# A layer of two mixtures of experts around attention: the first routing in written order, its slot sums in two PSUM banks, and one shared expert moved to another stage

## The chip, the cores and the metric

The kernel runs on one core of a Trainium2 chip. The metric is the device time of one execution in microseconds (us). Before the change three runs gave 1568.17, 1572.17 and 1578.36 us, so the median is 1572.17 us. Engines are named as the profile names them: PE multiplies matrices (PEld is its weight load), DVE does elementwise work and reductions, ACT evaluates functions and copies, POOL issues the gathers and the scatter-adds, and SP issues the other transfers.

## The reference, cut to what matters

The input is X of 4 sequences x 512 tokens x 512 values, all float32. The same mixture of experts (weights and router) is applied before and after an attention layer:

```python
x = L0_attn_X
x = x + 0.5 * _L0_ffn_ref(_layernorm(x, axis=-1), ...)
x = x + _L0_attn_ref(_layernorm(x, axis=-1), ...)
x = x + 0.5 * _L0_ffn_ref(_layernorm(x, axis=-1), ...)

# _L0_ffn_ref: 64 experts of width 192, each token in 6 of them
router_logits = x @ gate_w
topk_w, topk_ids = _grouped_topk(router_logits, bias)     # 8 groups of 8 experts; the best 4 groups, then the best 6
y = _routed_moe(x, topk_w, topk_ids, w_gate, w_up, w_down)
shared = jax.nn.silu(x @ ws_gate) * (x @ ws_up) @ ws_down
return (y + shared).reshape(orig_shape)
```

The reference's capacity is 2 * (512 * 6 // 64) = 96 slots for each expert. A token beyond an expert's 96th is dropped from it. The attention has 16 heads of 32 values and a rotary embedding of half of them.

## The kernel before, in words

**Stages.** Times are those of the profiled execution. First routing and most of the first shared expert (0 to 142 us); the first 32 pairs of experts (157 to 452); the rest of the first shared expert, then the projections to queries, keys and values; for each sequence b a *sums* stage (row maxima and sums of exponentials) and a *context* stage (probabilities times values), beside which run the projections of the next sequence and the second layer's routing of the one before; a last routing (1179 to 1229); the second 32 pairs of experts (to about 1542); a final addition.

**Routing (class `Route`).** A token tile is 128 tokens, a sequence has four. `begin` computes the layer norm's statistics of a sequence on DVE. `row` normalises a tile on ACT and stores it to `xn_d` in HBM; it has two buffers in the first routing. `turn` transposes the tile on PE and copies it on ACT, `score` multiplies it with the router's weights and takes a tanh on ACT (0.22 us). `choices` finds the experts of a whole sequence on DVE, in seven parts that a generator separates with `yield`; `choose` runs all seven. `count` finds each token's slot with two PE products (`pp`) and five DVE operations. `digits` compares the slot number's digits on DVE, giving tiles A and V for a pair of token tiles; in the first routing each has one buffer. `tokens` scales one half of V by the token's number with two ACT operations. `spread` multiplies A and V on PE into a bank `o` for each half of the groups (16 small products), and DVE adds the two into `acc`: index parts as they are, parts that say which pair of tiles it was times the pair's number. After eight pairs `finish` turns `acc` into the slot lists `en`, by which POOL gathers the experts' rows.

**Shared expert.** `gate` multiplies a tile with both input weights on PE (128x384, eight records of the trace), takes a tanh on ACT and two products on DVE (`product`); `turn_h` transposes the result on PE and copies it on ACT; `down` multiplies with the output weights on PE (`so`) and adds into x on DVE. `store` issues what waits to be stored.

**What sets the order.** PE's instructions stand in the order in which they are written. In the first routing only SP does so besides; ACT and DVE are ordered there by a scheduler. A list `steps` gives the places of the choices, counts and slot sums among the steps of the shared expert: in a loop over sequences g of 0 to 2 and five steps i, each step transposes tile i - 1's gate product, gates tile i, transposes and scores tile i of sequence g + 2, does what `steps` says, stores, issues one weight load and one clearing of the output (`some(1)`), and multiplies down tile i - 1. Weights of the first five pairs of experts (15 transfers of 768 KB) and 17 clearings of 256 KB and more are issued from this loop. The gathers wait for the rows, the routing weights and the cleared last rows of `xn_d`.

In the attention stages ACT and DVE are in written order as well. A list of pieces, each with a nominal cost, is worked off beside the 16 rounds of each stage:

```python
def long(self, keep=0):
    if sum(p[0] >= 1.0 for p in self.left) > keep:
        self.short()
        self.take()
```

A round of `sums` or `context` takes at most one piece of cost 1.0 or more, and up to two shorter ones around it; `sums` keeps two long pieces back, which `work.all()` runs behind the last round. `scored`, `gated` and `queued` give the pieces of the second layer's routing of a sequence: scores, the shared expert (four gates), and count with slot sums. Before the change `scored(b - 1)`, `gated(b - 1)` and `queued(b - 1)` run in context stages 1 and 2; those of the third sequence are in the fourth sums stage and, for `queued`, in the fourth context stage.

Of the kernel before, what the change touches and what calls it, by code (L numbers as in the profile page):

```python
# [9 lines left out]
F32 = mybir.dt.float32  # L10
# [7 lines left out]
P = 128  # L18
# [13 lines left out]
CAP = 96  # L32
# [50 lines left out]
def macaron_kernel(ctx: ExitStack, tc: tile.TileContext, X, ln_w, ln_b, W_in, W_out, gate_w, bias,  # L83
# [173 lines left out]
    class Route:  # L257


        def __init__(self, layer):  # L260
            self.layer = layer
            self.before_g = const.tile([P, E], BF, tag=f"before{layer}", name="before_g")
            nc.vector.memset(self.before_g, 0.0)

            self.acc = const.tile([CAP, G, 2 * SB, EG], BF, tag="acc", name="acc")
# [164 lines left out]
        def tokens(self, g, i):  # L430

            V = self.AV[g, i][1]
            for j, part in enumerate((part_1, part_2)):
                r = slice(j * G, (j + 1) * G)
                nc.scalar.activation(V[:, r, 0, :], V[:, r, 1, :], AF.Copy, scale=part)

        def spread(self, g, i, psum=None):

            (A, V), n, h = self.AV.pop((g, i)), 2, G // 2
            for k in range(2):  # L440
                o = (psum or self.psM).tile([P, 512], F32, tag="ps", name="o")
                ov = o[:CAP].rearrange("p (g w e) -> p g w e", g=h, e=EG)
                for q in range(h):
                    for j in range(n):
                        r = j * G + k * h + q
                        nc.tensor.matmul(ov[:, q].rearrange("p w e -> p (w e)"),
                                         lhsT=A[:, r].rearrange("p a e -> p (a e)"),
                                         rhs=V[:, r].rearrange("p w b -> p (w b)"), start=j == 0, stop=j == n - 1)
                to, pair = self.acc[:, k * h:(k + 1) * h], (g * TPB + i) // n
# [9 lines left out]
        def finish(self, psum=None):  # L459

            Z = self.rp.tile([CAP, 2, SB, G, EG], BF, tag="Z", name="Z", bufs=1)
            nc.vector.tensor_tensor(Z.rearrange("p v b g e -> p (v b) g e"), self.acc.rearrange("p g w e -> p w g e"),
                                    same.unsqueeze(1).unsqueeze(1).to_broadcast([CAP, 2 * SB, G, EG]), ALU.mult)
# [163 lines left out]
    with ExitStack() as s:  # L627
# [4 lines left out]
        with ExitStack() as f:  # L632
            rp = f.enter_context(tc.tile_pool(name="rp0", bufs=2))
            f.enter_context(tc.manual_schedule(engines={mybir.EngineType.SP}))
# [13 lines left out]
            route.use(rp, psA, psD, 2)  # L648
            route.xp = rp, 2 * TPB
            route.begin(0, xs[0])  # L650

            for t in range(2 * TPB + 1):
                g, i = divmod(t, TPB)
                if t == TPB - 1:
                    with tc.issue_after(route.begun):
                        route.begin(1, xs[1])
                if g < 2:
                    route.row(g, xs[g], i)
                    route.turn(g, i)
                if t > 0:  # L660
                    route.score(*divmod(t - 1, TPB))
                if t == TPB:
                    for later in range(2, B):
                        with tc.issue_after(route.begun):
                            route.begin(later, xs[later])
                    route.choose(0)
# [22 lines left out]
            steps = [lambda: route.choose(1), lambda: count(0), lambda: spread(0, 0), lambda: spread(0, 2), None,  # L689
                     lambda: (route.choose(2), count(1)), lambda: spread(1, 0), lambda: spread(1, 2), lambda: count(2),  # L690
                     None, lambda: (route.choose(3), spread(2, 0)), lambda: spread(2, 2), lambda: count(3),
                     lambda: spread(3, 0), lambda: spread(3, 2)]
            for g in range(B - 1):
# [33 lines left out]
    with ExitStack() as s:  # L727
# [167 lines left out]
        def gated(b):  # L895
# [5 lines left out]

            pieces = []
# [4 lines left out]
            return pieces  # L907

        def queued(b, chosen):

            def last():
                route.down(b, xs[b], TPB - 1)
# [10 lines left out]
            pieces = [(0.3, lambda: route.turn_h(b, TPB - 1)), (1.7, last)]  # L923
# [114 lines left out]
        for b in range(B):  # L1038
            if b > 0:
# [6 lines left out]
                else:  # L1046
                    work.add(pieces + [rest, rest] + early_rows(b - 1) + scored(b - 1, chosen) + gated(b - 1))
# [106 lines left out]
```

## Time and profile before

| | us |
|---|---|
| median of three runs | 1572.17 |
| profiled execution | 1571.97 |
| its span, first to last instruction | 1570.3 |
| PE busy | 1407.7 (90%) |
| DVE busy | 619.1 (39%) |
| ACT busy | 602.8 (38%) |
| POOL busy | 351.0 (22%) |
| mean granted clock of PE | 0.935 |
| routing's slot lists ready | 142.2 |
| first gather starts | 150.0 |
| first transpose of gathered rows | 157.35 |
| third context stage | 944.2 to 1031.3 |
| fourth sums stage | 1031.4 to 1120.8 |
| fourth context stage | 1121.3 to 1179.1 |

The span runs from the first to the last instruction of one profiled execution. Busy time counts each engine by itself; matrix products are pipelined, so a busy PE is not a PE at its peak. A row of instructions gives start, duration, engine, line, operation, tiles and count; in square brackets stands how long the engine sat idle before it and what ended that. A row of waits gives who waited for whom, the total, the number of times and the longest.

### The profile page before, as it was taken

How to read it: one execution, taken by the hardware profiler on the slowest of the kernel's cores; microseconds unless marked ns; L12 is line 12 of the kernel's file. 1: busy time of each engine (PE TensorE's matmuls, PEld its weight loads, DVE VectorE, ACT ScalarE, POOL GpSimd, SP SyncE). 2: the span in 40 equal slices, each digit the busy share in tenths (PEclk: the TensorE clock that was granted, in tenths of full speed). 3: DMA queues.
4: the chain of work that ended last, by engine and by line, in shares of the span. 5: the costliest groups of instructions: out<-in, count | busy, mean ns of one | idle time of the engine just before them, and what ended most of it. 6: DMA issues, size and time to landing. Idle time of an engine off the chain costs nothing.

```text
span 1570.3 us, 22935 instructions
## 1 busy us (share of the span) xinstructions
PE 1407.7 (90%) x9008; PEld 801.8 (51%) x9008; DVE 619.1 (39%) x1528; ACT 602.8 (38%) x1153; POOL 351.0 (22%) x321
## 2 busy tenths in 40 slices
PE   4785999999998999999899999998898799999990
PEld 4552877766653443334343334434334477777760
DVE  7575212221117566166144851465515412221110
ACT  4431112111112487568635775457562112121110
POOL 2001355554434000000000000000000245555535
PEclk9998899999998996999899998996998799999995
DMA  5377699999999300000000010000006489999989
GB/s 195 132 243 263 191 336 329 333 332 335 337 269 155 122 1 1 1 1 0 22 31 7 1 52 36 31 1 27 31 1 229 131 268 336 333 334 329 335 252 122
DMA packets 127035, 254.57 MB, mean 162 GB/s; under 512 B 15800, under 2 KB 32312, under 8 KB 126928
## 3 DMA queue, kind: packets, MB, share of 16 engines
q1 hardware_dynamic: 87216, 192.96, 35.0%
q0 software_dynamic: 39424, 59.97, 17.8%
q8 instruction: 72, 1.18, 0.3%
q14 instruction: 35, 0.29, 0.1%
q10 hardware_dynamic: 288, 0.16, 0.0%
HBM read 202.21 MB, written 56.95 MB: 165 GB/s over the span
## 4 chain that ended last, share of the span: by engine, by line
PE 55%; ACT 5%; DVE 4%; DMA 4%; issue 2%; POOL 1%; SPq 0%; POOLq 0%; ACTq 0%; DVEq 0%
PE pq L810 11%; PE gu L548 6%; PE sct L968 5%; PE sc L937 5%; PE cx L991 4%; PE sct L972 4%; PE ps_t L200 4%; PE po L859 3%; DMA w<-in_L_ffn_w_up_dram 3%; PE eo L567 3%; PE so L507 3%; PE gu L207 3%; PE gu L552 2%; PE eo L570 2%; ACT sc L945 1%
## 5 line engine op out<-in xcount | busy, mean ns | idle before, releaser
L525 POOL DMA_INDIRECT xr<-xn_d,en x128 | 119.7, 936 | 898.1 <-DVE sg L214 726.5
L548 PE MATMUL gu<-bT,w 128*128 128x96 f32 x2048 | 245.8, 278 | 9.4 <-DMA w<-in_L_ffn_w_up_dram 9.2
L548 PEld LDWEIGHTS gu<-bT,w 128*128 128x128 f32 x2048 | 238.5, 194 | 12.8 <-issue 12.7
L945 ACT ACTIVATE sc<-sc,nmq 128x512 f32<-128x512 f32 x256 | 168.9, 660 | 56.8 <-DVE nmq L940 51.1
L810 PE MATMUL pq<-w,lT 128*128 128x512 f32 x384 | 182.4, 623 | 5.5 <-ACT lT L201 2.7
L940 DVE TENSOR_REDUCE nmq<-sc 128x2 f32<-128x1024 f32 x128 | 151.3, 1221 | 76.9 <-PE sc L937 76.9
L575 POOL DMA_INDIRECT total<-ob,en x96 | 138.6, 1444 | 163.1 <-ACT ob L574 120.0
L574 ACT ACTIVATE ob<-eo,xr 96x512 f32<-96x512 f32 x128 | 80.6, 679 | 185.9 <-PE eo L570 182.6
L979 ACT ACTIVATE pT<-sct 128x1024 f32<-128x1024 f32 x128 | 124.2, 1022 | 63.7 <-PE sct L972 63.4
L559 DVE SCALAR_TENSOR_TENSOR sg<-sg,gu 128x288 f32<-128x288 f32 x64 | 29.1, 454 | 302.5 <-ACT sg L558 226.7
L558 ACT ACTIVATE sg<-gu 128x288 f32<-128x288 f32 x64 | 26.3, 411 | 314.8 <-PE gu L554 307.0
L567 PE MATMUL eo<-w,hT 128*96 128x512 f32 x256 | 125.3, 612 | 0.0
L810 PEld LDWEIGHTS pq<-w,lT 128*128 128x128 f32 x384 | 72.7, 198 | 97.7 <-issue 83.7
L201 DVE COPY bT<-ps_t 128x384 f32<-128x384 f32 x128 | 65.5, 552 | 136.1 <-PE ps_t L200 119.9
L937 PE MATMUL sc<-kT,qT 32*128 32x512 f32 x512 | 98.9, 720 | 12.7 <-ACT sc L945 12.0
L554 PE MATMUL gu<-bT,w 128*64 128x96 f32 x1024 | 98.7, 250 | 0.0
L552 PE MATMUL gu<-bT,w 128*64 128x96 f32 x1024 | 98.7, 250 | 0.0
L207 PE MATMUL gu<-wsgu,xT 128*128 128x384 f32 x256 | 94.4, 516 | 1.7 <-ACT ob L574 1.4
L968 PE MATMUL sct<-qT,kT 32*128 32x512 f32 x512 | 92.2, 664 | 3.1 <-ACT pT L979 3.1
L972 PE MATMUL sct<-nmT,pick 4*128 4x512 f32 x512 | 87.1, 629 | 5.1 <-ACT nmT L957 5.1
L552 PEld LDWEIGHTS gu<-bT,w 128*64 128x64 f32 x1024 | 86.7, 137 | 6.1 <-issue 0.2
L554 PEld LDWEIGHTS gu<-bT,w 128*64 128x64 f32 x1024 | 86.7, 137 | 0.0
(159 smaller groups left out, 1636.0 us busy)
## 6 DMA issues: line engine op xcount, KB each, us to landing
w<-in_L_ffn_w_gate_dram SPq DMA_DIRECT2D x64, 768.0 KB
w<-in_L_ffn_w_up_dram SPq DMA_DIRECT2D x64, 768.0 KB
w<-in_L_ffn_w_down_dram SPq DMA_DIRECT2D x64, 768.0 KB
total<-zero SPq DMA_DIRECT2D x39, 256.0 KB
xn_d<-xn SPq DMA_DIRECT2D x32, 256.0 KB
x<-in_L_attn_X_dram SPq DMA_DIRECT2D x16, 256.0 KB
x<-total POOLq DMA_DIRECT2D x16, 256.0 KB
out_dram<-x SPq DMA_DIRECT2D x16, 256.0 KB
```

The lines of the kernel that those rows point to most:

```text
L207: nc.tensor.matmul(gu[:rows, :2 * F].rearrange("p (w f) -> p w f", w=2), lhsT=bT[:, c, :], rhs=weights[:, :, c, :], start=c == 0, stop=c = ...
L548: nc.tensor.matmul(g[:, k, :], lhsT=w[:, k, c, f:f + P], rhs=x[:, c, :], start=c == 0, stop=c == DC - 1)
L552: nc.tensor.matmul(g[:FC, 2, :], lhsT=w[:, 0, c, P:F], rhs=xa[:, c, :], start=c == 0, stop=c == DC - 1)
L554: nc.tensor.matmul(g[FC:, 2, :], lhsT=w[:, 1, c, 0:FC], rhs=xb[:, c, :], start=c == 0, stop=c == DC - 1)
L567: nc.tensor.matmul(eos[k][:CAP], lhsT=hT[:, k, :], rhs=wd[:, 2 * k, :], start=True, stop=False)
L575: nc.gpsimd.indirect_dma_start(out=total[layer][k], in_=ob, in_offset=None, out_offset=bass.IndirectOffsetOnAxis(ap=en[:, e:e + 1], axis=0 ...
L810: nc.tensor.matmul(pq, lhsT=lTs[i][:, c, :], rhs=win[n][:, c, :], start=c == 0, stop=c == DC - 1)
L937: nc.tensor.matmul(scs[j // 2][:, j % 2, :], lhsT=qT[b][rows, c, q * P:(q + 1) * P], rhs=kT[b][rows, c, :], start=True, stop=True)
L940: nc.vector.tensor_reduce(nmv[:, q, 2 * pair:2 * pair + 2, c], scs[pair], AX.X, ALU.max, negate=True)
L945: nc.scalar.activation(scs[j // 2][:, j % 2, :], scs[j // 2][:, j % 2, :], AF.Exp, bias=nmq[:, q, j * DH + c:j * DH + c + 1], accum_out=sm ...
L968: nc.tensor.matmul(scs[j // 2][:, j % 2, :], lhsT=kT[b][rows, c, kt * P:(kt + 1) * P], rhs=qT[b][rows, c, :], start=True, stop=False)
L972: nc.tensor.matmul(scs[j // 2][:, j % 2, :], lhsT=pick[rows, c, :], rhs=nmT[b][rows, :], start=False, stop=True)
```

## The change

In the first routing ACT and DVE are put in written order too, and the order is written anew: all statistics first; rows one tile ahead; weight loads and clearings from the second tile on; in each step of the shared expert the gate without its products, the next sequence's transpose and score, then count (step 0) or slot sums (steps 1 and 2), then one part of the next choice, the gate's products, and another part. `count` and the slot sums of the last sequence stand behind the loop.

The slot sums of the first routing are held in the two banks of pool `psB`: a product of zeros opens each bank, the products of all eight pairs add to it, the pair's number is applied on ACT to the second half of V in `tokens`, and `finish` reads the two banks. `acc` is left to the second layer.

In the attention stages `gated` now ends with the last transpose and down projection, which were in `queued`. `gated(1)` moves from the third context stage to the fourth sums stage, where it takes the place of two empty pieces; two empty pieces stand ahead of `queued` in the second and third context stages.

```diff
-        def use(self, rp, psT, psM, xn_bufs, dig_bufs=1, last=False):
+        def use(self, rp, psT, psM, xn_bufs, dig_bufs=1, last=False, held=None):
...
+            self.sums = held and [held.tile([P, 512], F32, tag="ps", name="o") for _ in range(2)]
+            for o in self.sums or []:
+                nc.tensor.matmul(o[:CAP], lhsT=zero.bitcast(BF)[:, :CAP], rhs=zero.bitcast(BF)[:, :512], start=True, stop=False)
...
+            if self.sums:
+                nc.scalar.activation(V[:, :, 1, :], V[:, :, 1, :], AF.Copy, scale=float((g * TPB + i) // 2))
...
-                o = (psum or self.psM).tile([P, 512], F32, tag="ps", name="o")
+                o = self.sums[k] if self.sums else (psum or self.psM).tile([P, 512], F32, tag="ps", name="o")
...
+                                         start=j == 0 and not self.sums,
+                                         stop=j == n - 1 and (not self.sums or (pair, q) == (pairs - 1, h - 1)))
+                if self.sums:
+                    continue
...
+            for at, part in parts:
+                n = part.shape[1]
+                nc.vector.tensor_tensor(Z.rearrange("p v b g e -> p (v b) g e")[:, :, at:at + n, :],
...
-            f.enter_context(tc.manual_schedule(engines={mybir.EngineType.SP}))
+            f.enter_context(tc.manual_schedule(engines={mybir.EngineType.SP, mybir.EngineType.Activation, mybir.EngineType.DVE}))
...
-            route.use(rp, psA, psD, 2)
+            route.use(rp, psA, psD, 2, held=psB)
...
+            for g in range(B):
+                route.begin(g, xs[g])
+            route.row(0, xs[0], 0)
+            for t in range(2 * TPB + 1):
+                if t + 1 < 2 * TPB:
+                    g, i = divmod(t + 1, TPB)
+                    route.row(g, xs[g], i)
+                if t < 2 * TPB:
+                    route.turn(*divmod(t, TPB))
+                if t > 0:
+                    route.score(*divmod(t - 1, TPB))
+                    some(1)
+                if t == TPB:
+                    route.choose(0)
...
-                        route.gate(g, i)
+                        route.gate(g, i, 1)
                         if ahead:
                             route.turn(ahead, i)
                             route.score(ahead, i)
                             if i + 1 < TPB:
                                 route.row(ahead, xs[ahead], i + 1)
-                    step = steps.pop(0)
-                    if step:
-                        step()
+                        if i == 0:
+                            count(g)
+                        elif i < 3:
+                            spread(g, 2 * i - 2)
+                        choice(g + 1, 1)
+                        route.product(g, i)
+                        choice(g + 1, 1)
+                    if i > 0:
+                        route.down(g, xs[g], i - 1)
                     route.store()
                     some(1)
-                    if i > 0:
-                        route.down(g, xs[g], i - 1)
+            count(B - 1)
+            for i in range(0, TPB, 2):
+                spread(B - 1, i)
             route.finish()
...
-            return pieces
+            return pieces + [(0.3, lambda: route.turn_h(b, TPB - 1)), (1.7, last)]
...
-                    work.add(pieces + [rest, rest] + early_rows(b - 1) + scored(b - 1, chosen) + gated(b - 1))
+                    work.add(pieces + gated(b - 2) + early_rows(b - 1) + scored(b - 1, chosen) + gated(b - 1))
...
-                work.add(scored(b - 1, chosen) + gated(b - 1) + queued(b - 1, chosen))
+                work.add(scored(b - 1, chosen) + (gated(b - 1) if b == 1 else []) + [rest, rest] + queued(b - 1, chosen))
```

More of the change, by code (lines that the diff above doesn't have):

```diff
@@ L263, in __init__ @@
             nc.vector.memset(self.before_g, 0.0)
-            self.acc = const.tile([CAP, G, 2 * SB, EG], BF, tag="acc", name="acc")
+            self.acc = const.tile([CAP, G, 2 * SB, EG], BF, tag="acc", name="acc") if layer else None
             self.en = const.tile([CAP, E], U32, tag="en", name="en")
@@ L435, in tokens @@
                 nc.scalar.activation(V[:, r, 0, :], V[:, r, 1, :], AF.Copy, scale=part)
+            if self.sums:
+                nc.scalar.activation(V[:, :, 1, :], V[:, :, 1, :], AF.Copy, scale=float((g * TPB + i) // 2))
         def spread(self, g, i, psum=None):
             (A, V), n, h = self.AV.pop((g, i)), 2, G // 2
+            pair, pairs = (g * TPB + i) // n, NT // n
             for k in range(2):
-                o = (psum or self.psM).tile([P, 512], F32, tag="ps", name="o")
+                o = self.sums[k] if self.sums else (psum or self.psM).tile([P, 512], F32, tag="ps", name="o")
                 ov = o[:CAP].rearrange("p (g w e) -> p g w e", g=h, e=EG)
@@ L447, in spread @@
                                          lhsT=A[:, r].rearrange("p a e -> p (a e)"),
-                                         rhs=V[:, r].rearrange("p w b -> p (w b)"), start=j == 0, stop=j == n - 1)
-                to, pair = self.acc[:, k * h:(k + 1) * h], (g * TPB + i) // n
+                                         rhs=V[:, r].rearrange("p w b -> p (w b)"),
+                                         start=j == 0 and not self.sums,
+                                         stop=j == n - 1 and (not self.sums or (pair, q) == (pairs - 1, h - 1)))
+                if self.sums:
+                    continue
+                to = self.acc[:, k * h:(k + 1) * h]
                 index_o, which_o = ov[:, :, :SB], ov[:, :, SB:]
@@ L461, in finish @@
             Z = self.rp.tile([CAP, 2, SB, G, EG], BF, tag="Z", name="Z", bufs=1)
-            nc.vector.tensor_tensor(Z.rearrange("p v b g e -> p (v b) g e"), self.acc.rearrange("p g w e -> p w g e"),
-                                    same.unsqueeze(1).unsqueeze(1).to_broadcast([CAP, 2 * SB, G, EG]), ALU.mult)
+            parts = [(0, self.acc)] if not self.sums else [
+                (k * (G // 2), o[:CAP].rearrange("p (g w e) -> p g w e", g=G // 2, e=EG)) for k, o in enumerate(self.sums)]
+            for at, part in parts:
+                n = part.shape[1]
+                nc.vector.tensor_tensor(Z.rearrange("p v b g e -> p (v b) g e")[:, :, at:at + n, :],
+                                        part.rearrange("p g w e -> p w g e"),
+                                        same.unsqueeze(1).unsqueeze(1).to_broadcast([CAP, 2 * SB, n, EG]), ALU.mult)
             ps = (psum or self.psM).tile([P, 512], F32, tag="ps", name="slots")
@@ L647, in macaron_kernel @@
             route0 = route = Route(0)
-            route.use(rp, psA, psD, 2)
+            route.use(rp, psA, psD, 2, held=psB)
             route.xp = rp, 2 * TPB
[L650 to L666, printed above, removed]
             rest = [go for n in range(WS + WX) for go in load_pair(0, n, extra)]
@@ L687, in count, with choice @@
                 route.digits(g, 0)
[L689 to L692, printed above, removed]
+            def choice(g, n):
+                for _ in range(n):
+                    next(choices[g], None)
+            choices = {g: route.choices(g) for g in range(1, B)}
             for g in range(B - 1):
@@ L900, in part, with last @@
                 route.gate(b, i)
+            def last():
+                route.down(b, xs[b], TPB - 1)
+                route.store()
             pieces = []
@@ L906, in gated @@
                 pieces.append((4.3, lambda i=i: part(i)))
-            return pieces
+            return pieces + [(0.3, lambda: route.turn_h(b, TPB - 1)), (1.7, last)]
         def queued(b, chosen):
             def last():
-                route.down(b, xs[b], TPB - 1)
                 while work.later and work.later[0] in chosen:
@@ L921, in digits @@
                 route.digits(b, i)
-            pieces = [(0.3, lambda: route.turn_h(b, TPB - 1)), (1.7, last)]
+            pieces = [(1.7, last)]
             for i in (0, 2):
```

## The prediction

> **What bounds it now.** The profiled execution took 1571.97 us (span 1570.3), 0.2 below the median of the three runs, so I add to 1572.0. The chain of waits starts only in the last sequence's shared expert at 452.7 us, so the first routing is read from the table of stretches, from what PE waited for, and from instructions in order of time. In the stretches the columns are length, then busy time (instructions) of PE, weight load, DVE, ACT and POOL, then granted clock, DMA share and GB/s.
>
> ```profile
> 41.50:81.50 40.00, 31.60 (x141) 19.61 (x141) 23.98 (x93) 14.79 (x26) 0.00 (x0) 0.91 0.46 157
> 81.50:113.20 31.70, 27.17 (x142) 17.37 (x141) 22.00 (x72) 12.26 (x24) 0.00 (x0) 1.00 0.71 230
> 113.20:135.60 22.40, 19.75 (x102) 11.54 (x101) 20.17 (x75) 5.09 (x11) 0.00 (x0) 1.00 0.59 184
> 135.60:142.20 6.60, 3.93 (x31) 2.36 (x29) 5.56 (x13) 1.60 (x3) 0.00 (x0) 1.00 1.04 408
> ```
>
> From the first gate product (41.5) to the finished slot lists (142.2) are 100.7 us, of which PE is busy 31.60 + 27.17 + 19.75 + 3.93 = 82.45: the scheduler leaves PE only 18 us of waits. PE's waits in that stretch:
>
> ```profile
> PE o L446 <- DVE A L426: 6.8, 2, 5.0
> PE lg L307 <- ACT xT L201: 5.4, 8, 0.7
> PE o L446 <- ACT V L435: 3.3, 6, 1.1
> PE so L507 <- ACT hT L201: 1.0, 2, 0.5
> PE ps_t L200 <- DVE sg L214: 0.5, 1, 0.5
> ```
>
> PE never waits long for a gate product (0.5 us in all) or for token digits (1.1 at most). The lists are ready at 142.2, yet the gathers start at 150.0, when the last weights and clears have landed, and PE resumes 7.3 us later:
>
> ```profile
> 141.97 0.22 DVE L474 SCALAR_TENSOR_TENSOR en<-pt,none 96x64 uint32<-96x64 f32 x1
> ...
> 150.03 1.20 POOL L525 DMA_INDIRECT xr<-xn_d,en  x1 [133.12 <-DMA total<-zero]
> ...
> 157.35 3.12 PE L200 MATMUL ps_t<-ident,xr 96*128 96x96 f32 x16 [16.29 <-DMA xr<-xn_d,en]
> ```
>
> After that PE runs a pair of experts each 8.77 us, so a start later by X ends the stage later by X.
>
> **Part 1, up to 41.5: nothing.** DVE's statistics stand in the same order; PE's two added products of zeros (96x512) cost under 2 us, at 16.9, while tile 2 still waits for a store to land (21.97). Weights now start behind the third row store, at about 24 instead of 64.6; a step moves 768 + 256 + 256 KB, 3.3 us at the 400 GB/s of the last row above, for tiles that PE needs 2.45 us each for. The last of eight tiles then comes at 40 to 42, against 41.7. I take 0, bounds -2 and +3.
>
> **Part 1, the middle.** In the built program DVE and ACT keep the written order. For each of three sequences this makes these waits for PE, which before are hidden:
>
> (a) PE's order is gate of tile 0, one transpose and score, the count, then the transpose of tile 0's gate product. DVE's order is count (5 operations), digits V and A, the first 11 operations of the next choice, and only then that product. The last routing shows such rows unbroken:
>
> ```profile
> 1206.76 0.43 DVE L322 SCALAR_TENSOR_TENSOR sb<-lgs,bias_h 128x256 f32<-128x256 f32 x1 [7.53 <-ACT lgs L312]
> ...
> 1209.41 0.21 DVE L338 TENSOR_TENSOR grp<-m,m 128x32 f32<-128x32 f32 x1
> ...
> 1217.42 0.42 DVE L408 CAST q<-pp 128x256 int32<-128x256 f32 x1
> ...
> 1219.94 0.95 DVE L426 TENSOR_TENSOR A<-hv,digit_a 128x1536 bf16<-128x1536 bf16 x1
> ```
>
> Count and digits 1217.42 to 1220.89 = 3.5, choice 1206.76 to 1209.41 = 2.65, product 2 x 0.35 = 0.7: PE stands 6.9 us. Three times: 20.7.
>
> (b) In steps 1 and 2 ACT's order is score tanh 0.22, next row 1.29, two token scalings 1.33, and the new scaling of the whole second half (128x1024 bf16, not in the trace: between 0.66, the 128x512 row, and 1.33, two of them; I take 1.2, nearest the 1.02 of the 128x1024 exponential). PE's slot sums stand behind all of it: 4.1 us, four times; without row and score for the third sequence 0.33 + 2.5 = 2.8, twice. Together 22.
>
> (c) V and A have one buffer each. DVE's second digits (0.68 + 0.95) wait for the first slot sums and stand ahead of a choice part (1.1) and tile 1's product (0.7): 3.4, against 1.8 of down projection on PE: 1.6, three times, 4.8.
>
> End: the last sequence has no gate work beside it: count to V 2.7, tokens 2.5, sums 0.9, V 0.65 (behind those sums), tokens 2.5, sums 0.9, Z from two banks 1.4, slots 0.65, last DVE operations 1.1 = 13.3, of which 2.7 are PE work counted below: 10.6.
>
> The 32 additions into acc (0.41 each) go: DVE is busy 71.7 of the 100.7 us and not the bound, so this alone is worth only the last four in the end chain, already left out there.
>
> Sum: PE 82.45 less 2.0 (the half-clock stretch after one old wait) = 80.4; kept waits for xT 5.4 and hT 1.5; 20.7 + 22 + 4.8 + 10.6. That is 145.4 in place of 100.7, and the lists are ready at 187 at full clock.
>
> The clock comes on top. After the old 5.0 us wait PE ran half as fast:
>
> ```profile
> 66.02 0.34 PE L446 MATMUL o<-V,A 128*96 128x128 bf16 x1 [4.97 <-DVE A L426]
> 66.58 1.76 PE L446 MATMUL o<-V,A 128*96 128x128 bf16 x15 [0.22 <-ACT V L435]
> 68.13 3.12 PE L507 MATMUL so<-wsd,hT 96*128 96x512 f32 x4
> ```
>
> against 1.06 and 1.94 elsewhere, 2.0 us lost; a cold gate product took 5.34 against 2.75. After each (a) I add 2.6, after each 4.1 us wait 1.05, between 0 (after 1.84 us idle at 120.4 nothing was lost) and 2.1: 7.8 + 4.2 = 12; bounds 0 and nine times 2.6 = 23. Lists ready at 199.
>
> [...]
>
> Nothing then holds the gathers: the queue has been empty for long, since weights and clears are all issued by the third sequence. I give 5.5 us instead of 7.3 until PE resumes (bounds 4 and 7.3): 204.5 against 157.35, **+47**; bounds +31 (184 ready, 4) and +65 (215, 7.3).
>
> **Part 2.** Third context stage, with the second sequence's gates inside, then without:
>
> ```profile
> 975.50:1006.80 31.30, 31.30 (x158) 13.06 (x154) 13.15 (x48) 11.20 (x18) 0.00 (x0) 1.00 0.08 30
> 1006.80:1031.30 24.50, 23.95 (x187) 8.44 (x184) 8.86 (x19) 14.17 (x16) 0.00 (x0) 1.00 0.03 12
> ```
>
> Four rounds take 31.3, the next eight 24.5, 3.06 each: the gates cost 31.3 - 12.2 = 19.1, and PE was full, so they go whole; about 1 comes back where the count waits for choices now pressed into three rounds. In the fourth sums stage (1031.35 to 1120.8, 89.5) rounds are: 4 with projection 4.7; 5 with gates 4.2, 3 x 5.95 and 4.2; then 5.5, 4.0, 5.5, 5.5, 4.6, 4.5 and 4.5 (four exponentials 3.0 plus rows 1.29 and copies on ACT). That is 79.2 for 76.4: the old idle (13.0 us for two empty rounds, PE busy 6.28) is filled. But a round takes one long piece, so more is left behind the last round: three gates and four down projections in series instead of two and two. Each step is tanh 0.35, product 0.75, transpose 0.3, copy 0.45, down 1.9, gate 2.6 = 6.4; with the last exponentials 27.6 for the old 13.0. Net +17. The last context stage loses one transpose, one down projection and a wait, -3. The second one now ends with slot sums uncovered, +1.5. Part 2: -19 + 1 + 17 - 3 + 1.5 = **-3**; bounds -15 (tail half as bad) and +8.
>
> **Rivals.** (1) Forecast: 1572 + 47 - 3 = **1616**, chance 0.60. (2) Same waits, but the clock holds: 12 less, 1604; 0.17. For it: the 1.84 us wait; against: the 4.97 us one. (3) Waits half covered because ACT or DVE run earlier than I place them: half of 58 for the routing's new waits, no clock loss: 187 - 29 = 158 ready, gathers 8 late, PE maybe 2 quicker, with part 2 at -3: about 1575, within 1%; 0.14. (4) Other side: the queue's release. If the written order costs PE nothing, lists stand at 142, the gathers start 8 earlier and land 2 earlier, and with part 2 at -3 it is 1559, at -15 1547. It needs the new PE waits to stay under about 10 us; (a) alone is 20.7 and stands in the built order, so 0.09. (5) That only the banks act, acc's 13 us of DVE going: DVE is off the path, 1571, counted in (3).
>
> **Numbers.** Range 1588 (+31 - 15) to 1642 (+65 and +8, less 3 since both ends seldom meet). A measurement here tells 1% (about 16 us) from no change: slower 0.80, within 0.13, faster 0.07.
>
> **What would show it.** PE waiting some 7 us for sg from DVE three times, some 4 us for V from ACT at the slot sums, lists at 185 to 215, gathers right behind them; the third context stage near 69 us, the fourth sums stage over 100 with gate steps of 6.4 at its end. Wrong if DVE's products come before the count, or if the lists are ready before 160.

## The result, and the profile after

The changed kernel is **slower**: the ratio of its time to that of the kernel before is 1.033 (95% interval 1.024 to 1.042). Its profiled execution took 1623.56 us (span 1621.9) against 1571.97 (span 1570.3), 51.6 more. The four runs took 1623.56, 1630.71, 1648.63 and 1652.64 us, median 1639.67; the ratio leaves out the two longest, whose mean granted clock was 0.905 and 0.903 against 0.922 and 0.920.

**The first routing.** The table of stretches, from the first gate product on, one row for each sequence of the shared expert and one for the chain behind the loop (columns as before: length, then busy time (instructions) of PE, weight load, DVE, ACT and POOL, then granted clock, DMA share and GB/s):

```profile
41.85:96.42 54.57, 35.64 (x140) 21.55 (x141) 20.29 (x70) 16.34 (x28) 0.00 (x0) 0.81 0.47 154
96.42:147.85 51.43, 33.47 (x139) 20.66 (x138) 19.84 (x67) 13.78 (x25) 0.00 (x0) 0.80 0.40 132
147.85:186.20 38.35, 24.42 (x92) 13.54 (x91) 19.65 (x66) 7.34 (x14) 0.00 (x0) 0.87 0.29 93
186.20:203.00 16.80, 5.11 (x43) 4.58 (x41) 7.88 (x16) 4.78 (x6) 0.00 (x0) 0.57 0.04 16
```

From the first gate product to the gathers are 161.15 us (160.2 to the finished lists, against 100.7 before). PE is busy 98.64 of them, against 82.45: 16 us of the 60 are the same products at a lower clock, 44 are waits. No other engine is near its bound (DVE, the next, is busy 67.7). What PE waited for, in that stretch and the first rows of the experts:

```profile
PE o L453 <- ACT V L441: 28.8, 8, 5.5
PE ps_t L200 <- DVE grp L342: 21.6, 3, 7.9
...
PE lg L311 <- ACT xT L201: 5.4, 8, 0.7
...
PE ps_t L200 <- DVE sg L214: 2.3, 3, 1.1
```

The wait put down to `grp` is the one for tile 0's gate product: `grp` (L342) is the operation that stands behind that product on DVE. Rows in order of time show one wait of each kind and the clock behind it:

```profile
48.83 0.42 DVE L412 CAST q<-pp 128x256 int32<-128x256 f32 x1 [5.82 <-PE pp L409]
...
56.21 0.35 DVE L214 TENSOR_TENSOR sg<-sg,gu 128x192 f32<-128x192 f32 x1
...
56.71 0.63 PE L200 MATMUL ps_t<-ident,sg 128*96 128x128 f32 x2 [7.91 <-DVE grp L342]
...
57.13 5.32 PE L207 MATMUL gu<-wsgu,xT 128*128 128x384 f32 x8
...
67.22 1.06 ACT L441 ACTIVATE V<-V 128x1024 bf16<-128x1024 bf16 x1
68.33 1.86 PE L453 MATMUL o<-V,A 128*96 128x128 bf16 x16 [3.64 <-ACT V L441]
...
69.99 3.24 PE L523 MATMUL so<-wsd,hT 96*128 96x512 f32 x4
```

DVE goes from count to digits to the choice, 48.83 to 56.2, before it makes the product that PE has stood for since 48.8; 1.0 of it DVE itself waits, for a store, which makes this wait 7.91 where the other two are 6.82 and 6.83. The gate that follows takes 5.32 us in place of 2.75. Eleven us later ACT scales V behind the tanh and the row, PE waits 3.64, and the slot sums and the down projection again run at about half speed (1.06 and 1.94 elsewhere).

The lists and what follows them:

```profile
201.80 0.22 DVE L490 SCALAR_TENSOR_TENSOR en<-pt,none 96x64 uint32<-96x64 f32 x1
203.01 1.19 POOL L541 DMA_INDIRECT xr<-xn_d,en  x1 [186.46 <-DVE en L490]
...
206.66 0.87 PE L200 MATMUL ps_t<-ident,xr 96*128 96x96 f32 x4 [5.76 <-issue]
```

The gathers now wait for the lists and not for a queue; PE resumes 4.6 us behind the lists instead of 15.2. So the lists are 59.8 us late, PE's first transposes of gathered rows 49.3 (206.66 against 157.35), the experts' first product 50.8 (211.04 against 160.26) and the first product of the projections 50.1 (530.99 against 480.92): the experts give back less than 1.

**Part 2.** The third context stage, the fourth sums stage's rounds, and what is left behind its last round:

```profile
994.06:1064.55 70.49, 68.98 (x458) 27.18 (x458) 19.68 (x66) 39.88 (x47) 0.00 (x0) 0.90 0.04 14
1064.55:1145.00 80.45, 73.09 (x267) 33.90 (x265) 49.65 (x69) 54.38 (x140) 0.00 (x0) 0.83 0.07 27
1145.00:1175.60 30.60, 23.63 (x64) 11.10 (x63) 9.76 (x26) 8.50 (x19) 0.00 (x0) 0.90 0.07 27
```

By the first score product of each stage, the whole difference comes apart so:

| stretch | before | after | difference |
|---|---|---|---|
| start to third context stage | 940.60 | 990.51 | +49.9 |
| third context stage | 90.75 | 74.04 | -16.7 |
| fourth sums stage | 89.96 | 111.04 | +21.1 |
| fourth context stage, to its last product | 57.85 | 54.74 | -3.1 |
| last projection and routing, to the second experts | 69.53 | 68.25 | -1.3 |
| second experts and end | 321.6 | 323.3 | +1.7 |
| span | 1570.3 | 1621.9 | +51.6 |

So part 1 costs 50 us and part 2, in this execution, 1.

### The profile page after: what moved, and what is told of

It reads as the page before. It is cut to its first block, busy times and chain, and to the rows that moved or that the text cites. A ratio compares the mean times of both kernels' runs of the same rounds, so it can differ in the third digit from the quotient of the medians.

```text
span 1621.9 us, 22914 instructions
## 1 busy us (share of the span) xinstructions
PE 1426.5 (88%) x9010; PEld 813.3 (50%) x9010; DVE 615.8 (38%) x1497; ACT 609.1 (38%) x1161; POOL 350.7 (22%) x321
## 4 chain that ended last, share of the span: by engine, by line
PE 55%; ACT 5%; DVE 3%; DMA 2%; issue 2%; POOL 1%; POOLq 0%; SPq 0%; ACTq 0%; DVEq 0%
PE pq L834 10%; PE gu L564 6%; PE sct L995 5%; PE sc L964 5%; PE sct L999 4%; PE cx L1018 4%; PE ps_t L200 4%; PE eo L583 3%; PE po L883 3%; PE gu L207 3%; PE so L523 3%; PE gu L568 2%; PE eo L586 2%; DMA w<-in_L_ffn_w_up_dram 1%; ACT sc L972 1%
## 5 line engine op out<-in xcount | busy, mean ns | idle before, releaser
L207 PE MATMUL gu<-wsgu,xT 128*128 128x384 f32 x256 | 99.9, 540 | 1.7 <-ACT ob L590 1.4
L995 PE MATMUL sct<-qT,kT 32*128 32x512 f32 x512 | 96.1, 664 | 3.3 <-ACT pT L1006 3.3
L999 PE MATMUL sct<-nmT,pick 4*128 4x512 f32 x512 | 91.0, 629 | 5.1 <-ACT nmT L984 5.1
## 6 DMA issues: line engine op xcount, KB each, us to landing
w<-in_L_ffn_w_gate_dram SPq DMA_DIRECT2D x64, 768.0 KB, 15.4
```

What stands on the lines that cost most here:

```text
L207: nc.tensor.matmul(gu[:rows, :2 * F].rearrange("p (w f) -> p w f", w=2), lhsT=bT[:, c, :], rhs=weights[:, :, c, :], start=c == 0, stop=c = ...
L995: nc.tensor.matmul(scs[j // 2][:, j % 2, :], lhsT=kT[b][rows, c, kt * P:(kt + 1) * P], rhs=qT[b][rows, c, :], start=True, stop=False)
L999: nc.tensor.matmul(scs[j // 2][:, j % 2, :], lhsT=pick[rows, c, :], rhs=nmT[b][rows, :], start=False, stop=True)
```

## Experiments

The theory: PE's waits for the gate product on DVE (a) and for the scaled V on ACT (b), with the clock that they lower, are the loss. The rival: something else that comes as late holds PE, and takes over when one of these is removed.

**DVE's product first.** In the changed kernel:

```diff
-                        route.gate(g, i, 1)
+                        route.gate(g, i)
...
-                        choice(g + 1, 1)
-                        route.product(g, i)
-                        choice(g + 1, 1)
+                        choice(g + 1, 2)
```

> The changed kernel with DVE's two operations of the gate product placed right behind the gate, ahead of count, slot sums and both parts of the choice; nothing else moves. Theory: it takes away the three waits of 7.91, 6.82 and 6.83 us behind which PE stood for tile 0's product (21.6 us), the half-speed gates behind them (5.32, 5.09 and 4.38 for 2.75, so 7 us), and the waits of (c), 2.3 us: about 30 less than the changed kernel, 1594, lists ready near 173. Rival: the product was only the last of several things that were late, and PE then waits as long for the slot sums or a copy from ACT: above 1612.

Measured: ratio to before 1.027 (1.017 to 1.036), profiled execution 1602.60, first transposes of gathered rows at 183.01 in place of 206.66. PE's waits in the same stretch:

```profile
PE o L453 <- ACT V L441: 22.5, 6, 5.5
...
PE o L453 <- DVE sg L213: 3.7, 1, 3.7
PE o L453 <- DVE sy L380: 2.7, 1, 2.7
```

The three waits for tile 0 are gone. The eight waits at the slot sums are left as they were: the profile puts two of them down to DVE, and together they are 28.9 us, against 28.8. The gathered rows come 23.65 us earlier, not 30: the clock fell behind these waits instead (behind one of 3.66 a down projection took 3.72, where it had taken 3.24). Another 3 us are lost later, where the second context stage took 93.5 for 90.5, of which more below.

**ACT's scalings first.** In the changed kernel, without the move above:

```diff
             def spread(g, i):
-                route.tokens(g, i)
                 route.spread(g, i)
...
+                        if 0 < i < 3:
+                            route.tokens(g, 2 * i - 2)
                         route.gate(g, i, 1)
...
             for i in range(0, TPB, 2):
+                route.tokens(B - 1, i)
                 spread(B - 1, i)
```

> The changed kernel with ACT's three scalings of V in steps 1 and 2 issued ahead of the gate's tanh, instead of behind the score's tanh and the next row; the last sequence's, behind the loop, stay. Theory: the six waits for V at the slot sums (3.64 x 4 and 2.72 x 2, 20.0 us) go, and with them the half-speed slot sums and down projections behind them (3.8 and 5.1 us); since a warm down projection covers less, the waits of (c) grow by 3 to 4 us: about 25 less than the changed kernel, 1598. Rival: the scalings, 2.35 us, now delay the gate's tanh and by it the product, and PE waits there instead: above 1612.

Measured: ratio 1.014 (1.009 to 1.020), profiled execution 1599.26, first transposes at 182.90.

```profile
PE ps_t L200 <- DVE grp L342: 21.6, 3, 8.0
PE o L453 <- ACT V L441: 9.0, 3, 5.5
...
PE ps_t L200 <- DVE sg L214: 5.3, 3, 1.8
```

The six waits for V in the loop shrink to one of 0.2; the two behind the loop stay; (c) grows by 3.0, as forecast, since a down projection at full speed covers less.

**Both.**

> The changed kernel with both moves: DVE's gate products right behind the gate, and ACT's scalings of V ahead of the gate's tanh. Theory: the two moves each brought the lists 23.7 us forward (to 176) and act on different waits, so together 47: lists at 152 to 154, gathers right behind, and 1577 when no half-speed stretch falls into the context stages. Rival: with both gone the next late thing decides (digits of the second pair behind the slot sums, DVE's choice): lists at 165 or later, above 1588.

Measured: ratio 1.0019 (0.9997 to 1.0040). The slot product, PE's last product ahead of the lists, starts at 150.17 (199.89 in the changed kernel: 49.7 earlier, more than the 23.7 and 23.8 of the single moves), the first transposes at 156.92 against 157.35 before the change. So two moves in the order of lines, with nothing computed less, take back all that part 1 cost; the rival is out. The slot product still stands 9.7 us later than before the change (140.46); that is made up because PE resumes 6.75 us behind it, where it was 16.9. What PE still waits for:

```profile
PE o L453 <- ACT V L441: 10.9, 4, 5.5
PE lg L311 <- ACT xT L201: 9.3, 8, 2.7
```

**Only the idle time filled.** To separate the waits from the clock:

```diff
+            def warm(n):
+                for j in range(n):
+                    nc.tensor.matmul(route.sums[j % 2][:CAP], lhsT=zero.bitcast(BF)[:, :CAP],
+                                     rhs=zero.bitcast(BF)[:, :512], start=False, stop=False)
...
                 route.tokens(g, i)
+                warm(8)
                 route.spread(g, i)
...
+                    if i == 1:
+                        warm(14)
                     if i > 0:
                         route.turn_h(g, i - 1)
```

> The changed kernel with products of zeros added to the held banks (96x512, they change no sum) where PE would stand idle: 14 ahead of each first transpose of a gate product, 8 ahead of each pair's slot sums. No wait is shortened; only the idle time is filled. Theory of the clock: the gates, slot sums and down projections behind the waits run at full speed; these cost 6.5 + 3.8 + 5.1 = 15.4 us in the changed kernel, of which 2 to 3 come back as waits of (c): 13 less, 1610 (1606 to 1614). Rival: the clock was low there for another reason, or what is lost is hidden in the next wait: 1622 to 1626, more if the fillers outlast the waits.

Measured: first transposes at 199.69, 7.0 earlier. Rows in order of time:

```profile
48.19 3.18 PE L696 MATMUL o<-zero 128*96 128x512 bf16 x14
56.96 5.13 PE L207 MATMUL gu<-wsgu,xT 128*128 128x384 f32 x8
64.14 1.89 PE L696 MATMUL o<-zero 128*96 128x512 bf16 x8
67.96 1.05 PE L453 MATMUL o<-V,A 128*96 128x128 bf16 x16 [1.93 <-ACT V L441]
68.85 1.94 PE L523 MATMUL so<-wsd,hT 96*128 96x512 f32 x4
```

Where eight products filled half of a 3.64 us wait or more of one of 2.72, slot sums and down projection ran at full speed. That holds at all six places in the loop, five of which ran slow in the changed kernel: of their 8.9 us of half speed nothing is left, and (c) took 3.0 back. Fourteen products took only 3.2 us, the gate product still kept PE waiting, and the gates behind it still took 5.13, 4.44 and 5.33. So the clock does follow these waits at the slot sums. Of the forecast 13 us about half came; at (a), where 3.8 to 5.2 us of each wait were left, nothing was gained, so there the link is not shown. The profiled execution as a whole took 1630.59, because its second context stage lasted 105.8 us in place of 90.5; two others took 1615.27 and 1615.82, less than any of the changed kernel's. The ratio to before is 1.027 (1.021 to 1.033), which overlaps the changed kernel's.

**ACT and DVE back to the scheduler.**

```diff
-            f.enter_context(tc.manual_schedule(engines={mybir.EngineType.SP, mybir.EngineType.Activation, mybir.EngineType.DVE}))
+            f.enter_context(tc.manual_schedule(engines={mybir.EngineType.SP}))
```

> The changed kernel with ACT and DVE given back to the scheduler in the first routing; PE and SP keep the new written order, the sums stay in the two banks. Theory: what costs is the written order of ACT and DVE, so (a) and (b) go as in the kernel before; what stays is the last sequence behind the loop, a chain of 11 to 13 us: lists at 152 to 156 by the trace. Rival: PE's new order (counts one step earlier, choices spread out, banks) sets the waits whoever orders ACT and DVE: lists above 180.

Only the first routing of its profiled execution (1603.97 us) is read, since two context stages ran at half speed in it; the other run took 1577.11. Slot product at 148.84, first transposes at 155.62: with PE's new order, the banks and the early weights kept, the written order of ACT and DVE is what costs 51 us.

**Part 1 alone, part 2 alone.** The changed kernel with the attention pieces of before, and the kernel before with the changed pieces.

> The changed kernel with part 2 undone: its first routing, and the attention stages of the kernel before. Theory: the first routing costs what the trace of the changed kernel shows up to the first weights of the projections, 50 us, and nothing gives it back later: 1572 + 50 = 1622, gathers as in the changed kernel at 203. Rival: the 50 us are shortened later (weights and rows of the experts are loaded ahead, so the experts stage could run faster when it starts late): below 1610.

> The kernel before with part 2 alone: the pieces of the attention stages as in the changed kernel, the first routing untouched. If the stages can be read one by one from the two traces (third context stage -16.7, fourth sums stage +21.1, fourth context stage -3.1, second context stage 0), this takes 1573 to 1575 us, within 0.3% of before, and the lists are ready at 142 as before. If my size for part 2 holds (-3), 1569. Rival: part 2 carries a good part of the 51.6 us, because the first routing's delay would have been absorbed later; then this is above 1585.

Part 1 alone: ratio 1.037 (1.032 to 1.043), profiled execution 1631.29. The projections start 48.6 later than before (50.1 in the changed kernel), and the experts give nothing back; 15.3 more lie in the second context stage. Part 2 alone: ratio 1.012 (1.007 to 1.017), all four runs 1588.67 to 1595.45, where I had 1569 or 1574. That number is on the rival's side, but not for the rival's reason, since part 1 alone shows that its delay is not absorbed later. By stages: second context 105.8 for 90.5, third 90.1 where the changed kernel took 74.0, fourth sums stage +21.1, fourth context -3.4. The second context stage holds the same pieces in the same order as before, up to its last gate. Here it is up to the first gate, and behind it, first of the kernel before and then of part 2 alone:

```profile
760.39:795.00 34.61, 31.20 (x186) 13.36 (x185) 3.07 (x12) 20.39 (x27) 0.00 (x0) 0.80 0.08 31
795.00:850.90 55.90, 55.37 (x346) 21.56 (x342) 21.57 (x67) 25.41 (x34) 0.00 (x0) 1.00 0.06 22
```

```profile
756.50:804.50 48.00, 44.60 (x185) 18.21 (x184) 4.51 (x16) 21.32 (x28) 0.00 (x0) 0.54 0.06 22
804.50:862.30 57.80, 57.12 (x342) 23.34 (x338) 19.73 (x60) 24.67 (x33) 0.00 (x0) 0.97 0.06 21
```

The same products (185 and 186 records) take 34.6 us in one and 48.0 in the other. Both fall to half speed some 4 us into the stage; the kernel before is back 16.4 us in, during the routing's first score product, part 2 alone only in the first gate, at 804.61:

```profile
802.75 1.94 PE L994 MATMUL cx<-pT,v 128*32 128x512 f32 x8
804.61 4.59 PE L207 MATMUL gu<-wsgu,xT 128*128 128x384 f32 x8
809.14 1.14 PE L971 MATMUL sct<-qT,kT 32*128 32x512 f32 x8
```

From 767 to 804 PE worked there without a pause. The two spans differ by 23.4 us: the two long half-speed stretches are 31.4 of it (15.3 and 16.1), part 2's own pieces come to +1.0 (-16.7, +21.1, -3.4), and stages with the same pieces at another clock to -9.0. Whether the whole change is slower than part 1 alone can't be told (1.033 against 1.037, with overlapping intervals). As a program of its own, part 2 costs about 1.2%, and none of its four executions was free of the loss; that its own pieces are worth only +1 is read from stages without these stretches, and why they come here was not found.

**The wait at the start of a context stage filled.** Ten products of zeros ahead of the first picks, once in the kernel before and once with part 2 alone:

```diff
+                for _ in range(10 if (c, kt) == (0, 0) else 0):
+                    nc.tensor.matmul(scs[0][:, 0, :], lhsT=zero.bitcast(BF)[:, :P],
+                                     rhs=zero.bitcast(BF)[:, :S], start=False, stop=False)
                 for j in range(HG):
                     rows = slice(j * DH, j * DH + NC)
```

> The kernel before with ten products of zeros (128x512, added to the first scores, which they don't change) ahead of the first picks of each context stage, where PE stands 2.4 us for ACT's copy of the row maxima. Theory of the clock: that wait halves the clock, and the score products behind it, which use 32 and 4 of the 128 rows, don't bring it back for some 10 us at best (before: picks 2.09 for 1.04 at 763.95, full speed again at about 777); without it the second and third context stages each lose 5 to 6 us and the first and last 0 to 2: about 12 less, 1560. Rival: the clock falls for these stages' own products, not for the wait: no change, 1572.

> Part 2 alone, with the same products of zeros ahead of the first picks. Theory: part 2 itself is worth about +1, and the 20 us that it measured are two half-speed stretches of 35 us, in the second and in the third context stage, which the wait sets off and which nothing ends because the 128-row products come late or, in the third, have gone: with the wait filled this takes 1561, within 0.3% of the kernel before with the same products; second context stage (first scores to the next stage's) near 87 against 105.8, third near 70 against 90.1. Rival: the half speed comes from the order of the pieces themselves: above 1585 still.

Measured: 1.007 (1.003 to 1.011) and 1.005 (1.003 to 1.007) of before. Both are slower than before, where I had some 12 us less, so my theory of what lowers the clock there falls. The rivals (no change in the first, above 1585 in the second, whose median was 1581.87) did not come as stated either. In the kernel before with the products:

```profile
765.65 2.10 PE L971 MATMUL sct<-zero 128*128 128x512 bf16 x9 [0.16 <-issue]
767.94 1.14 PE L975 MATMUL sct<-nmT,pick 4*128 4x512 f32 x8 [0.18 <-ACT nmT L957]
...
772.66 1.22 PE L968 MATMUL sct<-qT,kT 32*128 32x512 f32 x2 [1.94 <-ACT pT L982]
```

The picks (`sct<-nmT,pick`) run at full speed, but behind the wait for the first exponentials, 0.99 before and 1.94 now, the scores run at half speed all the same. In the first context stage there was hardly a wait to fill (0.29); the products added 2.1 us there, and the stage took 57.9 for 54.5. With part 2 the two stages took 92.9 and 76.1 in place of 105.8 and 90.1; but the products also moved the moment at which the stage begins, so this does not show that they did it.

**Weights early in the kernel before.** To measure the queue's release by itself:

```diff
...
                 if t > 0:
                     route.score(*divmod(t - 1, TPB))
+                    some(1)
...
```

Left out above: `some` and its two lists are defined ahead of this loop instead of behind it.

> The kernel before with one change in the first routing: one weight load and one clearing are issued behind each of the first eight scores, as in the changed kernel, instead of from the shared expert's steps on; ACT and DVE stay with the scheduler. Theory of the queue's release: the gathers start right behind the lists (142) instead of at 150, and PE resumes 6.8 us behind its slot product as in the changed kernel, where it was 16.9: first transposes of gathered rows near 149 against 157.35, about 8 less than before, 1564. Rival: the earlier loads push back something that PE needs before 41.5 or the rows' stores, and the lists are late by as much: 1572 or more.

Measured: ratio 1.003 (1.000 to 1.007). The release is there: the gathers start at 152.90, 1.2 us behind the start of the last list operation, as in the changed kernel. But the lists are late, as the rival said. The first gate product starts at 46.80 instead of 41.51, and the scheduler's one long wait has grown from 5.0 to 10.8:

```profile
PE o L446 <- DVE A L426: 12.6, 2, 10.8
```

Slot product at 150.18 against 140.46, first transposes at 156.55 against 157.35: the 8 us are worth less than 1 in this order.

**A written order without the waits.** Gate products first; V scaled behind the gate's tanh; choices, counts and sums placed so that the third sequence's steps cover the last sequence's; attention as before the change. `pairs`, `counts` and `parts` say at which step (g, i) the slot sums of a pair, a count and parts of a choice stand (against the changed kernel):

```diff
+            counts = {(0, 0): 0, (0, 3): 1, (1, 2): 2, (2, 2): 3}
+            pairs = {(0, 1): (0, 0), (0, 2): (0, 2), (1, 0): (1, 0), (1, 1): (1, 2), (1, 3): (2, 0), (2, 0): (2, 2),
+                     (2, 3): (3, 0), (2, 4): (3, 2)}
+            parts = {(0, 0): (1, 2), (0, 1): (1, 3), (0, 2): (1, 3), (0, 4): (2, 2), (1, 0): (2, 3), (1, 1): (2, 3),
+                     (1, 4): (3, 2), (2, 0): (3, 3), (2, 1): (3, 3)}
...
+                    if i < TPB:
+                        route.gate(g, i)
+                        if ahead:
+                            route.turn(ahead, i)
+                    if at in pairs:
+                        route.tokens(*pairs[at])
...
+                    if at in pairs:
+                        spread(*pairs[at])
+                    if at in parts:
+                        choice(*parts[at])
+                    if 0 < i < TPB:
+                        route.down(g, xs[g], i - 1)
```

> A first routing in written order without the waits: gate products first; scalings of V behind the gate's tanh and the copy of the transposed tile; choices, counts and slot sums spread so that the last sequence's count and sums stand in the third sequence's steps, as in the kernel before; held banks and early weights as in the changed kernel; attention stages as in the kernel before. Theory: with both moves the lists stood at 150.2 plus the last DVE steps, 9 to 11 of it the last sequence's chain behind the loop, which now has gates and down projections beside it: slot product at 139 to 142, gathers right behind, first transposes at 146 to 149 against 157.35, so 8 to 11 less than before: 1562 to 1565, lower than both kernels. Rival: DVE's choices, now pressed into fewer steps, become late for the count or the gate product: first transposes above 154, 1570 or more.

Measured: ratio 1.000 (0.997 to 1.003). Slot product at 146.45, first transposes at 152.82, 4.5 earlier than before: neither theory nor rival. Later stages took this back (second context stage 93.4 for 90.5, fourth sums stage 93.1 for 90.0). PE's eight slot sums still waited for V, 0.3 to 2.7 us each, 11.9 in all, and the clock fell behind some of them. So the last run moves them behind the down projection of their step (against the run above):

```diff
+                    if at in pairs and i == 0:
+                        route.tokens(*pairs[at])
...
-                    if at in pairs:
+                    if at in pairs and i > 0:
                         route.tokens(*pairs[at])
...
-                    if i == TPB:
-                        route.down(g, xs[g], i - 1)
                     if at in counts:
                         count(counts[at])
+                    if i > 0:
+                        route.down(g, xs[g], i - 1)
                     if at in pairs:
                         spread(*pairs[at])
                     if at in parts:
                         choice(*parts[at])
-                    if 0 < i < TPB:
-                        route.down(g, xs[g], i - 1)
```

> The interleaved first routing with PE's slot sums moved behind the down projection of their step, and, where a step has no down projection (step 0), the scalings of V ahead of the gate's tanh. Theory: the eight waits for V (1.21 x 5, 2.73, 2.72 and 0.34, 11.9 us) are covered by the down projection's 1.94 us, and the half-speed products behind them (slot sums 1.84 and 1.86, down projections 2.86, 3.72 and 2.65, a gate of 3.15) run at full speed: 12 to 16 less on PE up to the slot product; first transposes of gathered rows at 138 to 143 against 152.8, 1556 to 1562. Rival: DVE's choices stand behind the additions of the down projections and the digits, so that count or gate products become late, or the last routing weights land too late for the gathers: first transposes above 149, 1567 or more.

Measured: ratio **0.990** (0.986 to 0.994), profiled execution 1558.63: 1% less than the kernel before, with an interval clear of 1. PE's waits of the first routing and the first gather:

```profile
PE lg L311 <- ACT xT L201: 5.4, 8, 0.7
PE ps_t L200 <- DVE sg L214: 3.5, 2, 2.1
PE o L453 <- ACT V L441: 1.7, 2, 1.0
```

```profile
136.45 1.19 POOL L541 DMA_INDIRECT xr<-xn_d,en  x1 [119.61 <-DVE en L490]
```

First transposes at 140.11, 17.2 earlier than before; the projections start 16.4 earlier, and some 3 of it are lost again in the fourth sums stage (93.1 for 90.0, at a granted clock of 0.76 for 0.79). Nothing but the lists holds the gathers here, 13.6 us earlier than before.

## Why the prediction was right, and where its steps were off

The forecast was 1616 and the profiled execution 1623.56; the likeliest case is the one that came, and the waits are those that it named. That the lists came within 3 us of the forecast is partly luck: (b) and (c) were forecast 4.5 too long, the clock's share and the chain behind the loop 5.9 too short. Point by point:

- **Up to 41.5:** nothing, and the first gate product came 0.3 later.
- **(a):** 20.7 forecast, 21.6 measured, of which 1.0 is DVE's own wait for a store; the moved product removed it whole.
- **(b):** 22 forecast, 20.0 measured (3.64 x 4 and 2.72 x 2). The new scaling took 1.06, not the 1.2 I took. How much of (b) belongs to that scaling and so to the banks was not tried by itself; the order alone removed it.
- **(c):** 4.8 forecast, 2.3 measured. The size was off because I priced the cover at a full-speed down projection, 1.8, while the one behind a wait for V takes about 3. Where the clock was kept up, it was 5.3.
- **The clock:** 12 forecast. In the changed kernel the three gates cost 6.5 more, the slot sums 3.8 and the down projections 5.1: 15.4, within the bounds and above the value. In the chain behind the loop the slot sums and the slot product ran at half speed as well, 2.0 of the 2.5 us by which it was longer than forecast (15.8 from the count, not 13.3). One wait of the kernel before, 3.86 us at 1059.4, tells nothing of what waits do to the clock: the granted clock was 0.50 from 1056.97 on, and the score products ahead of that wait, at 1057.29, already took 2.08 us in place of 1.13.
- **Lists, gathers, experts:** lists at 199 forecast, 202 measured; gathers right behind; PE resumes +47 forecast, +49.3 measured (+50.1 at the projections). That no queue holds the gathers was right.
- **Part 2:** -3 forecast, +1.3 in this execution; this is the step that was wrong in sign. The third context stage gave 16.7 and not 18, the second did not lose the 1.5 that I had put on it, the fourth gave 3.1 for 3. The mis-sized term is the fourth sums stage: +17 forecast, +21.1 measured, 80.45 for 79.2 in its rounds and 30.6 for 27.6 behind them. The gate steps took 6.70 for my 6.4, and the first gate (4.23) and the last down projection (3.67) ran at a low clock, which I had not counted there.
- **The rivals:** that the clock holds is refuted by the rows and, at the slot sums, by the filled waits. That the waits are half covered is refuted by (a) and (b). The other side, the queue's release, exists (gathers 1.2 us behind the start of the last list operation instead of 8.1), but needs lists as early as before, and it was the last run, with another order, that had them. That only the banks act is refuted by the time; with the scheduler back and the banks kept, the slot product stood at 148.8.

What the prediction lacked is the spread. Four executions of the changed kernel lie between 1623.56 and 1652.64. Between the traces of different kernels, differences of this size are half-speed stretches of the context stages, some 15 us each; whether the same stretches separate executions of one program is not shown, since each program has one trace. The profiled executions of both kernels had short ones, and for that the closeness of 1616 to 1623.56 owes something to luck.

## What to carry to other kernels

When an engine is put in written order, list for each of its operations who waits for it, and write those with a waiting PE first: two moves in the order brought the experts' start forward by 49.7 us, with the same work done. A short piece of independent work of the waiting engine in front of the consumer covers the wait without a faster producer: with a down projection of 1.9 us ahead of the slot sums their waits fell from 11.9 to 1.7 us, and they ran at full speed. Compare kernels stage by stage before putting a difference of the whole down to an edit: a stage whose own work the edit didn't touch moved by 15 us.

## What the runs showed of the hardware that I had not expected

**Half speed comes in steps of 3.41 us, and what sets their number stays open.** In the traces of the kernel before and of the changed kernel the granted clock is 1.00 or 0.50, and every change of it inside the span lies a whole number of 3.41 us from the others: the stretches at 0.50 last 3.41 us to 30.72 us (9 steps, 1117.08 to 1147.80 in the changed kernel). In the second context stage the clock was low from 763.42 to 777.08 in the kernel before and from 813.29 to 826.94 in the changed kernel, 13.65 us or 4 steps each. The instructions of this stage up to the first gate are the same in all kernels but the two with products of zeros in it. Yet the stretch at half speed, worked out from the rows that took twice their time, was longer in others: 15 to 21 us with both moves, in the interleaved order and in the last run, about 44 with ACT and DVE back to the scheduler, and about 48 in three (part 1 alone, part 2 alone, the idle time filled). What decides between them was not shown.

With part 2 alone PE was busy 44.60 of 48.00 us at a granted clock of 0.54. Of the 185 products there 96 use 32 or 4 of the 128 rows, but the other 89 (context, the router's scores, transposes) use all 128, so products of few rows alone don't account for it. The stretches of about 44 and 48 us ended in the first gate product each time (it took 4.48 to 4.61 us in place of 2.75), the kernel before's in a score product of the router (776.70: 1.27 us); in the third context stage of part 2 alone the half speed ended at about 1002 without either.

**The length of a wait does not decide.** Behind 2.41 us products took twice their time in the kernel before (763.95: 2.09 us) and ran at full speed with both moves (763.38: 1.14). In the changed kernel slot sums behind 2.72 us took 1.86 (165.17) and 1.05 (176.28); in the interleaved order they took 1.84 (54.86) and 1.05 (87.22) behind 1.21. Behind 1.93 us with eight products of zeros ahead of it (67.96 above) they kept full speed.
